# Attention with a condition, one core: the last step's scores move ahead of step 30's sums, and GpSimd adds half of them

## The chip, the core and the metric

The kernel runs on one core of a Trainium2 chip. Five engines work side by side, each through its own instructions in order, and wait for one another by semaphores: TensorE (PE in the profile, its weight loads PEld), VectorE (DVE), ScalarE (ACT), GpSimd (POOL) and SyncE (SP, which only issues DMAs). TensorE writes its results to PSUM, eight banks of 512 float32 columns; all else lies in SBUF. The metric is the device time of one execution in microseconds.

## The reference

For 8 sequences of 512 tokens and 512 features, 16 heads of 32 features each; everything is float32:

```python
Q, K, V = heads(x @ Wq.T + bq), heads(x @ Wk.T + bk), heads(x @ Wv.T + bv)
cQ = Q + heads(cond @ Wq.T + bq)
cK = K + heads(cond @ Wk.T + bk)
attn = softmax(cQ @ cK.T / sqrt(32))
out = x + merge(attn @ V)
```

A step of the kernel, `t` from 0 to 31, is one sequence and one group of four heads. For each it needs the scores, their row maxima, the exponentials, the sums of the exponentials (the softmax's denominators), the product of the exponentials with V, the division, and the addition of x.

## The kernel before

Only the last two steps bear on the change: `t = 30` and `t = 31`. Their scores are computed with the keys in the partitions. One call of `exponentials(t, kc, at)` makes the scores of one key block `kc` (128 keys, four heads j = 0 to 3, 512 queries): on TensorE four short matmuls that put minus the row maximum into four banks (L753, from the tile `maxT`), four that add keys times queries (L756), and on ScalarE four exponentials (L766), bank by bank in the order of `at`, into two buffers of `store`, one for heads 0 and 1 and one for heads 2 and 3. `crossed` (L1287) does the same for key blocks 0 to 2 of step 30 and makes maxima of step 31 in between; there the buffer of heads 2 and 3 is filled first.

`times_v(t, kc, pt)` multiplies such a block with V into one bank, four heads side by side (L824). The denominators need the sum of the exponentials over all keys. `sum_of(t, acc, kc, on, prs)` adds the buffers of key blocks elementwise on the engine `on`: for `kc = 1` block 0 plus block 1 (L1277), for `kc = 2` and `3` the tile `acc` plus that block (L1279). `prs` says which half, `[0]` (heads 0 and 1) or `[1]` (heads 2 and 3); one half is 128 x 1024 float32. `times_ones(acc, pd, ...)` then sums over the partitions by a matmul with ones (L850).

Step 31 can only begin once its row maxima stand as three bf16 parts in `split`: VectorE makes them by `split_max` (L715 to L718, 128 x 16 each), TensorE turns them (L737), VectorE copies them to `maxT` (L743). Behind that, each engine works in the order in which the code is written: TensorE takes turns between `exponentials` and `times_v`, VectorE runs the additions, ScalarE the exponentials.

At the very end, step 31's denominators and product are multiplied out on VectorE, turned on TensorE, divided, and sent out by two DMAs (L1442 to L1468). Step 30's result takes another way: the partial products are added in `parts` (L1403), VectorE turns the denominators (L1416) and the result (L1421), multiplies by the reciprocal (L1423), GpSimd adds x (L1424), and four DMAs send it (L1429).

The PSUM bank numbers in `at` matter as far as a bank that is to be written must have been read before.

Of the kernel before, what the change touches and what calls it, by code (L numbers as in the profile page):

```python
# [9 lines left out]
F32 = mybir.dt.float32  # L10
# [7 lines left out]
def kernel(  # L18
# [38 lines left out]
    nc = tc.nc  # L57
    P = 128
# [19 lines left out]
    op = ctx.enter_context(tc.tile_pool(name="op", bufs=2))  # L78
# [37 lines left out]
    def banks(i, n=1):  # L116

        row = row_of[0] or [at_end[j] for j in TURNS[turn[0]]]
        j = row[i]
        if n == 1:  # L120
            return psum[:, j, :]
        k = row[i + 1]
        return psum[:, j : k + 1 : k - j, :]

    def bank_of(i):
        return psum[:, at_end[i], :]
# [32 lines left out]
    BL = 32  # L159
    NB = S // BL  # L160
# [56 lines left out]
    def chunk():  # L217

        ring_at[0] += 1
        return store[:, places[(ring_at[0] - 1) % len(places)]]  # L220
# [366 lines left out]
    def open_max(t):  # L587
        if t not in nmax:
            nmax[t] = op.tile([P, NS, HG, 1], F32, tag="nmax", name=f"nmax_{t}", bufs=3)
            sums[t] = op.tile([P, NS, HG, 1], F32, tag="sums", name=f"sums_{t}", bufs=3)  # L590
# [48 lines left out]
    def row_scores(t, qc, j, pt):  # L639
        r = slice(j * HD, (j + 1) * HD)  # L640
        nc.tensor.matmul(  # L641
            pt,
            qkT["q", t][r, qc * P : (qc + 1) * P],
            qkT["k", t][r, :],
            start=True,
            stop=True,
        )

    def row_max_of(t, qc, pr, pt):
        nc.vector.tensor_reduce(  # L650
            nmax[t][:, qc, pr * 2 : pr * 2 + 2, 0], pt, AX.X, ALU.max, negate=True
        )
# [56 lines left out]
    def split_max(t, on=nc.gpsimd):  # L709

        if t >= T:
            return
        m, sp = nmax[t], split[t % 2]
        rest = op.tile([P, NS, HG, 1], F32, tag="rest", name=f"rest_{t}")
        on.tensor_copy(sp[:, :, :, 0:1], m)  # L715
        on.tensor_tensor(rest, m, sp[:, :, :, 0:1], ALU.subtract)
        on.tensor_copy(sp[:, :, :, 1:2], rest)
        on.tensor_tensor(sp[:, :, :, 2:3], rest, sp[:, :, :, 1:2], ALU.subtract)  # L718
# [29 lines left out]
    def exponentials(t, kc, at=None):  # L748

        bank = [bank_of(i) for i in at] if at else [banks(i) for i in range(HG)]  # L750
        for j in range(HG):
            r = slice(j * HD, j * HD + 3)
            nc.tensor.matmul(bank[j], onesb[r, :], maxT[t][r, :], start=True, stop=False)  # L753
        for j in range(HG):
            r = slice(j * HD, (j + 1) * HD)
            nc.tensor.matmul(  # L756
                bank[j],
                qkT["k", t][r, kc * P : (kc + 1) * P],
                qkT["q", t][r, :],
                start=False,  # L760
                stop=True,
            )
        for pr in range(NP):
            e = es[t, kc, pr] = chunk()
            for i in range(2):
                nc.scalar.activation(e[:, i, :], bank[pr * 2 + i], AF.Exp)  # L766
# [54 lines left out]
    def times_v(t, kc, pt, chunks=range(NS)):  # L821
        b, g = divmod(t, G)
        for j in range(HG):
            nc.tensor.matmul(  # L824
                pt[j * HD : (j + 1) * HD, :],
                vs[b % 2][:, kc, (g * HG + j) * HD : (g * HG + j + 1) * HD],
                es[t, kc, j // 2][:, j % 2, :],
                start=(kc == chunks[0]),
                stop=(kc == chunks[-1]),
            )  # L830
# [17 lines left out]
    def times_ones(of, pt, start, stop):  # L848
        for j in range(HG):
            nc.tensor.matmul(  # L850
                pt[j * HD : (j + 1) * HD, :],
                ones[:, :HD],
                of[j // 2][:, j % 2, :],
                start=start,
                stop=stop,
            )
# [100 lines left out]
    bank = bank_of  # L957
# [88 lines left out]
    parts = {}  # L1046

    def late_part(i):
        return late[0][:, i, :]
# [224 lines left out]
    def sum_of(t, to, kc, on, prs=range(NP)):  # L1274
        for pr in prs:
            if kc == 1:
                on.tensor_tensor(to[pr], es[t, 0, pr], es[t, 1, pr], ALU.add)  # L1277
            else:
                on.tensor_tensor(to[pr], to[pr], es[t, kc, pr], ALU.add)  # L1279

    def room_for_sums(t):
        a = stage.tile([P, NC, D], F32, tag="w", name=f"acc_{t}")
        return [a[:, pr * 2 : pr * 2 + 2, :] for pr in range(NP)]

    def row(i):
        turn[0] = 8 + i

    def crossed(t, kc, qc, u=None):


        u = u or t + 1
        open_max(u)
        bank = [banks(i) for i in range(HG)]

        def maxima(js):
            for j in js:
                row_scores(u, qc, j, banks(HG + j))

        def scores(js):
            for j in js:  # L1300
                r = slice(j * HD, j * HD + 3)
                nc.tensor.matmul(bank[j], onesb[r, :], maxT[t][r, :], start=True, stop=False)
            for j in js:
                r = slice(j * HD, (j + 1) * HD)
                nc.tensor.matmul(
                    bank[j],
                    qkT["k", t][r, kc * P : (kc + 1) * P],
                    qkT["q", t][r, :],
                    start=False,
                    stop=True,  # L1310
                )

        maxima((0, 1))
        scores((2, 3))
        scores((0, 1))
        maxima((2, 3))
        for pr in (1, 0):
            e = es[t, kc, pr] = chunk()
            for i in range(2):
                nc.scalar.activation(e[:, i, :], bank[pr * 2 + i], AF.Exp)  # L1320
        for j in range(2):
            nc.vector.tensor_reduce(
                nmax[u][:, qc, j : j + 1, 0], banks(HG + j), AX.X, ALU.max, negate=True
            )
        row_max_of(u, qc, 1, banks(HG + 2, 2))

    t = T - 3
# [46 lines left out]
    t = T - 2  # L1374
# [10 lines left out]
    acc = room_for_sums(t)  # L1385
    sum_of(t, acc, 1, nc.gpsimd, [1])
    part_of(t, banks(2), [0])
    row(2)
    crossed(t, 2, 3)
    split_max(t + 1, nc.vector)  # L1390
    pa, rest = banks(2), [1, 2, 3]
    times_v(t, 1, pa, rest)
# [2 lines left out]
    transpose_max(t + 1, bank(5), nc.vector.tensor_copy)  # L1395
    times_v(t, 2, pa, rest)
    sum_of(t, acc, 1, nc.vector, [0])
    sum_of(t, acc, 2, nc.vector)

    t = T - 1  # L1400
    exponentials(t, 0, (2, 3, 0, 1))
    times_v(t - 1, 3, pa, rest)
    nc.vector.tensor_tensor(parts[t - 1], pa, parts[t - 1], ALU.add)  # L1403
    sum_of(t - 1, acc, 3, nc.vector)
    exponentials(t, 1, (7, 4, 5, 2))
    pv = bank(3)
    times_v(t, 0, pv)
    acc2 = room_for_sums(t)
    sum_of(t, acc2, 1, nc.vector)
    exponentials(t, 2, (0, 1, 7, 6))  # L1410
    times_v(t, 1, pv)
    pd = bank(5)
    times_ones(acc, pd, True, True)
    sum_of(t, acc2, 2, nc.vector)
    den = late_part(3).rearrange("p (f e) -> p f e", e=BL)
    nc.vector.transpose(den.rearrange("p f e -> p (f e)"), pd)  # L1416

    rec = op.tile([P, NB, 1], F32, tag="recs", name=f"recs_{t - 1}")
    nc.vector.reciprocal(rec, den[:, :, 0:1])
    y30 = op.tile([P, NB, BL], F32, tag="res", name=f"res_{t - 1}")  # L1420
    nc.vector.transpose(y30.rearrange("p f e -> p (f e)"), parts[t - 1])  # L1421
    x30 = xr.pop(t - 1)
    nc.vector.tensor_tensor(y30, y30, rec.broadcast_to([P, NB, BL]), ALU.mult)  # L1423
    nc.gpsimd.tensor_tensor(y30, y30, x30, ALU.add)  # L1424
# [1 line left out]
    def store_30(queue, hs):  # L1426
        b, g = divmod(t - 1, G)
        for h in hs:
            queue.dma_start(spread(out[b], g * P + h * BL), y30[h * BL : (h + 1) * BL])  # L1429

    store_30(nc.sync, (0, 1))
    exponentials(t, 3, (4, 2, 0, 1))
    times_v(t, 2, pv)
    pd = bank(7)
    times_ones(acc2, pd, True, False)
# [66 lines left out]
```

## Time and profile before

| | us |
|---|---|
| median of 3 runs | 649.41 (649.35 to 650.63) |
| the profiled execution | 649.67 |
| its span in the trace | 647.80 |
| PE busy in the span | 641.7 (99%) |
| DVE busy | 600.3 (93%) |
| ACT busy | 533.5 (82%) |
| POOL busy | 409.9 (63%) |

The change touches only the last 25 us or so of the span, so that stage's own rows matter more than these shares. Of matmuls the profile models the end; they are pipelined, and two groups that follow each other overlap by a tenth or two of a microsecond in its rows.

### The profile page before, as it was taken

How to read it: one execution, taken by the hardware profiler on the slowest of the kernel's cores; microseconds unless marked ns; L12 is line 12 of the kernel's file. 1: busy time of each engine (PE TensorE's matmuls, PEld its weight loads, DVE VectorE, ACT ScalarE, POOL GpSimd, SP SyncE). 2: the span in 40 equal slices, each digit the busy share in tenths (PEclk: the TensorE clock that was granted, in tenths of full speed). 3: DMA queues.
4: the chain of work that ended last, by engine and by line, in shares of the span. 5: the costliest groups of instructions: out<-in, count | busy, mean ns of one | idle time of the engine just before them, and what ended most of it. 6: DMA issues, size and time to landing. Idle time of an engine off the chain costs nothing. (4 is left out here: it accounts for less than half of the span.)

```text
span 647.8 us, 24814 instructions
## 1 busy us (share of the span) xinstructions
PE 641.7 (99%) x9856; PEld 357.3 (55%) x9856; DVE 600.3 (93%) x845; ACT 533.5 (82%) x1364; POOL 409.9 (63%) x651
## 2 busy tenths in 40 slices
PE   9999999999999999999999999999999999999997
PEld 8445555556555555555555555555655555555541
DVE  3799999999999999999999999999999999999887
ACT  2479888889888889888888988898988888898564
POOL 3633655686765775668576776568767577675650
PEclk9999999999999999999999999999999999999999
DMA  7615588888978788877878978878898767796831
GB/s 191 107 26 85 128 164 171 172 171 191 180 158 172 161 180 175 183 165 164 185 171 174 198 150 185 165 173 169 180 195 158 156 144 163 159 189 149 192 63 34
DMA packets 248457, 102.02 MB, mean 157 GB/s; under 512 B 229962, under 2 KB 230474, under 8 KB 248340
## 3 DMA queue, kind: packets, MB, share of 16 engines
q1 hardware_dynamic: 234196, 65.54, 53.6%
q0 software_dynamic: 12384, 33.83, 20.3%
q8 instruction: 78, 1.28, 0.8%
q10 hardware_dynamic: 1760, 1.05, 0.5%
q14 instruction: 39, 0.32, 0.2%
HBM read 19.75 MB, written 8.39 MB: 43 GB/s over the span
## 5 line engine op out<-in xcount | busy, mean ns | idle before, releaser
L593 DVE TENSOR_REDUCE nmax<-psum 128x1 f32<-128x512 f32 x279 | 177.6, 675 | 9.2 <-PE psum L641 4.9
L701 ACT ACTIVATE psum<-psum,nmax 128x512 f32<-128x512 f32 x248 | 165.1, 678 | 3.6 <-DVE nmax L593 3.0
L641 PE MATMUL psum<-kT,qT 32*128 32x512 f32 x1024 | 162.0, 613 | 0.0
L701 ACT ACTIVATE store<-psum,nmax 128x512 f32<-128x512 f32 x204 | 139.5, 700 | 25.0 <-DVE nmax L593 24.8
L682 POOL DMA_DIRECT2D store<-store x258 | 128.6, 503 | 47.2 <-DMA store<-store 28.8
L799 ACT ACTIVATE store<-psum 128x512 f32<-128x512 f32 x232 | 119.8, 603 | 33.4 <-PE psum L785 33.4
L660 DVE STREAM_TRANSPOSE store<-store 128x1024 f32<-128x1024 f32 x116 | 138.9, 1217 | 0.0
L650 DVE TENSOR_REDUCE nmax<-psum 128x2 f32<-128x1024 f32 x98 | 118.9, 1213 | 0.0
L840 PE MATMUL psum<-store,v 128*32 128x256 f32 x1856 | 106.8, 381 | 0.2 <-ACT store L1320 0.2
L840 PEld LDWEIGHTS psum<-store,v 128*32 128x32 f32 x1856 | 57.3, 110 | 57.2 <-ACT wT_q L632 21.2
L913 POOL TENSOR_TENSOR res<-res,recs 128x512 f32<-128x512 f32 x30 | 31.3, 1045 | 90.8 <-DVE res L912 90.8
L785 PE MATMUL psum<-qT,kT 32*128 32x256 f32 x928 | 83.8, 374 | 0.0
L641 PEld LDWEIGHTS psum<-kT,qT 32*128 32x128 f32 x1024 | 61.6, 184 | 35.4 <-issue 17.8
L785 PEld LDWEIGHTS psum<-qT,kT 32*128 32x128 f32 x928 | 60.9, 184 | 5.6 <-issue 0.3
L701 ACT ACTIVATION_READ_ACCUMULATOR psum<-psum,nmax 128x1 f32 x248 | 55.1, 222 | 0.0
L203 POOL TENSOR_TENSOR xr<-xr,bvs 128x512 f32<-128x512 f32 x30 | 38.4, 1282 | 15.6 <-DMA x<-in_x_dram 12.8
L462 PE MATMUL psum<-wc_v,xc 128*32 128x256 f32 x768 | 47.7, 379 | 0.0
L462 PE MATMUL psum<-xc,wc_q 128*32 128x256 f32 x720 | 44.7, 379 | 0.0
L462 PE MATMUL psum<-xc,wc_k 128*32 128x256 f32 x720 | 44.5, 379 | 0.0
L701 ACT ACTIVATION_READ_ACCUMULATOR store<-psum,nmax 128x1 f32 x204 | 44.4, 217 | 0.0
L914 POOL TENSOR_TENSOR res<-res,xr 128x512 f32<-128x512 f32 x30 | 38.3, 1277 | 2.3
L462 PE MATMUL psum<-xT,wT_k 128*32 128x256 f32 x480 | 34.5, 382 | 0.0
(191 smaller groups left out, 972.5 us busy)
## 6 DMA issues: line engine op xcount, KB each, us to landing
store<-store SPq DMA_DIRECT2D x264, 128.0 KB, 2.6
store<-store POOLq DMA_DIRECT2D x258, 128.0 KB, 3.8
out_dram<-res SPq DMA_DIRECT2D x122, 64.0 KB, 3.6
xr<-in_x_dram SPq DMA_DIRECT2D x120, 64.0 KB, 4.4
x<-in_x_dram SPq DMA_DIRECT2D x112, 64.0 KB, 3.3
w_q<-in_L_cond_Wq_dram SPq DMA_DIRECT2D x4, 256.0 KB, 3.9
w_v<-in_L_cond_Wv_dram SPq DMA_DIRECT2D x16, 64.0 KB, 2.5
w_k<-in_L_cond_Wk_dram SPq DMA_DIRECT2D x16, 48.0 KB, 2.6
```

Source lines behind the costliest of these rows:

```text
L203: nc.gpsimd.tensor_tensor(xr[t], xr[t], bias, ALU.add)
L462: nc.tensor.matmul(pt[r], still[:, r], moving, start=(kc == kcs[0]), stop=(kc == kcs[-1]))
L593: nc.vector.tensor_reduce(nmax[t][:, qc, j : j + 1, 0], pt, AX.X, ALU.max, negate=True)
L641: nc.tensor.matmul(pt, qkT["q", t][r, qc * P : (qc + 1) * P], qkT["k", t][r, :], start=True, stop=True,)
L650: nc.vector.tensor_reduce(nmax[t][:, qc, pr * 2 : pr * 2 + 2, 0], pt, AX.X, ALU.max, negate=True)
L660: nc.vector.transpose(e, e)
L682: (nc.gpsimd if here else nc.sync).dma_start(to, of)
L701: nc.scalar.activation(to, of, AF.Exp, bias=nmax[t][:, qc, j, :], accum_out=sums[t][:, qc, j, :],)
L785: nc.tensor.matmul(banks(j)[:, i * HS : (i + 1) * HS], qkT["k", t][r, kc * P : (kc + 1) * P], qkT["q", t][r, KQ * P :], start=False, stop= ...
L799: nc.scalar.activation(e[:, j], banks(j), AF.Exp)
L840: nc.tensor.matmul(pt[j * HD : (j + 1) * HD, half * HS : (half + 1) * HS], vs[b % 2][:, kc, (g * HG + j) * HD : (g * HG + j + 1) * HD], e, ...
L914: nc.gpsimd.tensor_tensor(y, y, xr.pop(t), ALU.add)
```

## The change

Four things change in the last two steps.

1. Of step 30's additions `kc = 2` and `kc = 3`, the half `[1]` moves from VectorE to GpSimd, which already made that half of `kc = 1`. VectorE keeps the half `[0]` and makes it right behind its other additions of step 30.
2. The transposition of step 30's result (`y30`) moves on VectorE from behind the denominators' to right behind the addition of `parts`.
3. On TensorE (and so for ScalarE) the scores of the last key block, `exponentials(t, 3)` of step 31, move ahead of step 30's sums with ones and of the product `times_v(t, 2)`; step 30's sums with ones stand behind them.
4. The banks change with it: the last scores go to (4, 5, 2, 0) instead of (4, 2, 0, 1), step 30's sums to bank 1 instead of 5.

```diff
     part_of(t, banks(2), [0])
     row(2)
     crossed(t, 2, 3)
+    sum_of(t, acc, 2, nc.gpsimd, [1])
     split_max(t + 1, nc.vector)
     pa, rest = banks(2), [1, 2, 3]
     times_v(t, 1, pa, rest)
...
     transpose_max(t + 1, bank(5), nc.vector.tensor_copy)
     times_v(t, 2, pa, rest)
     sum_of(t, acc, 1, nc.vector, [0])
-    sum_of(t, acc, 2, nc.vector)
+    sum_of(t, acc, 2, nc.vector, [0])
+    sum_of(t, acc, 3, nc.vector, [0])
+    sum_of(t, acc, 3, nc.gpsimd, [1])
 
     t = T - 1
     exponentials(t, 0, (2, 3, 0, 1))
     times_v(t - 1, 3, pa, rest)
     nc.vector.tensor_tensor(parts[t - 1], pa, parts[t - 1], ALU.add)
-    sum_of(t - 1, acc, 3, nc.vector)
+    y30 = op.tile([P, NB, BL], F32, tag="res", name=f"res_{t - 1}")
+    nc.vector.transpose(y30.rearrange("p f e -> p (f e)"), parts[t - 1])
     exponentials(t, 1, (7, 4, 5, 2))
     pv = bank(3)
     times_v(t, 0, pv)
...
     exponentials(t, 2, (0, 1, 7, 6))
     times_v(t, 1, pv)
-    pd = bank(5)
+    sum_of(t, acc2, 2, nc.vector)
+    exponentials(t, 3, (4, 5, 2, 0))
+    pd = bank(1)
     times_ones(acc, pd, True, True)
-    sum_of(t, acc2, 2, nc.vector)
     den = late_part(3).rearrange("p (f e) -> p f e", e=BL)
     nc.vector.transpose(den.rearrange("p f e -> p (f e)"), pd)
 
     rec = op.tile([P, NB, 1], F32, tag="recs", name=f"recs_{t - 1}")
     nc.vector.reciprocal(rec, den[:, :, 0:1])
-    y30 = op.tile([P, NB, BL], F32, tag="res", name=f"res_{t - 1}")
-    nc.vector.transpose(y30.rearrange("p f e -> p (f e)"), parts[t - 1])
     x30 = xr.pop(t - 1)
...
     store_30(nc.sync, (0, 1))
-    exponentials(t, 3, (4, 2, 0, 1))
     times_v(t, 2, pv)
```

What stands in VectorE's row before, from the parts of step 31's maxima to the product of step 30's result with its reciprocal (`acc_8444` is step 30's sum, `acc_8540` step 31's, `x2` both halves):

```order
L715 CAST split<-nmax_8338 128x16
L716 TENSOR_TENSOR rest_8471<-nmax_8338,split 128x16
L717 CAST split<-rest_8471 128x16
L718 TENSOR_TENSOR split<-rest_8471,split 128x16
L743 COPY maxT_8496<-psum 128x512
L1277 TENSOR_TENSOR acc_8444<-store 128x1024
L1279 TENSOR_TENSOR acc_8444<-acc_8444,store 128x1024 x2
L1403 TENSOR_TENSOR parts<-psum,parts 128x512
L1279 TENSOR_TENSOR acc_8444<-acc_8444,store 128x1024 x2
L1277 TENSOR_TENSOR acc_8540<-store 128x1024 x2
L1279 TENSOR_TENSOR acc_8540<-acc_8540,store 128x1024 x2
L1416 STREAM_TRANSPOSE store<-psum 128x512
```

And the same place in the changed kernel, from the copy to `maxT` on (`acc_8542` is now step 31's sum, `res_8524` step 30's result):

```order
L743 COPY maxT_8497<-psum 128x512
L1277 TENSOR_TENSOR acc_8444<-store 128x1024
L1279 TENSOR_TENSOR acc_8444<-acc_8444,store 128x1024 x2
L1406 TENSOR_TENSOR parts<-psum,parts 128x512
L1408 STREAM_TRANSPOSE res_8524<-parts 128x512
L1277 TENSOR_TENSOR acc_8542<-store 128x1024 x2
L1279 TENSOR_TENSOR acc_8542<-acc_8542,store 128x1024 x2
L1421 STREAM_TRANSPOSE store<-psum 128x512
```

Five additions of step 30 have become three, all of the half `[0]`, and the transposition of the result stands ahead of step 31's additions.

GpSimd's row at its end, in the changed kernel, from the result of step 29 (`res_8417`) on; before, the row of L1279 was not there:

```order
L913 TENSOR_TENSOR res_8417<-res_8417,recs_8415 128x512
L914 TENSOR_TENSOR res_8417<-res_8417,xr_8143 128x512
L1277 TENSOR_TENSOR acc_8444<-store 128x1024
L1279 TENSOR_TENSOR acc_8444<-acc_8444,store 128x1024 x2
L1427 TENSOR_TENSOR res_8524<-res_8524,store 128x512
```

The two additions stand where GpSimd had nothing between L1277 and step 30's last addition.

## The prediction

> **What bounds the kernel now.** I read the page's shares first, then the chain of work that ended last, then the timeline of each engine in the last 25 us, where the change lies.
>
> ```profile
> PE 641.7 (99%) x9856; PEld 357.3 (55%) x9856; DVE 600.3 (93%) x845; ACT 533.5 (82%) x1364; POOL 409.9 (63%) x651
> ```
>
> TensorE is busy for nearly the whole span. So a wait that puts TensorE back before its last work is paid in full, unless a later wait swallows it. The chain, in order of time (start, length, what), says where TensorE isn't the bound:
>
> ```profile
> 638.23 1.24 DVE acc L1279
> 639.47 0.04 issue
> 639.51 1.48 PE psum L850 x10
> ```
>
> Its last passage from VectorE to TensorE is VectorE's last addition of step 31 (L1279, `kc = 2`, half `[1]`), which releases the sums with ones (L850). From there to the end the chain is a fixed sequence. TensorE's timeline shows that wait (start, length, what):
>
> ```profile
> 634.47 1.07 PE L824 MATMUL psum<-store,v 128*32 128x512 f32 x8
> 635.36 1.04 PE L850 MATMUL psum<-acc,ones 128*32 128x512 f32 x8
> ...
> 637.52 1.07 PE L824 MATMUL psum<-store,v 128*32 128x512 f32 x8
> 638.40 1.73 PE L850 MATMUL psum<-acc,ones 128*32 128x512 f32 x6
> 639.52 0.62 PE L850 MATMUL psum<-store,ones 128*32 128x512 f32 x2
> ...
> 640.82 0.60 PE L850 MATMUL psum<-store,ones 128*32 128x512 f32 x2
> ```
>
> A group of eight starts 0.88 after the one before (637.52 to 638.40) and takes 1.04. The sums of step 31 are two groups, so without a wait they would end at 638.40 + 0.88 + 1.04 = 640.32. They end at 640.82 + 0.60 = 641.42: VectorE costs **1.1 us** here. That is all that a faster VectorE can give, as TensorE's timeline has no gap from L737's turning (627.59, below) to 638.40.
>
> VectorE in the same stretch has no idle time that matters until the sums are there:
>
> ```profile
> 628.09 0.42 DVE L743 COPY maxT<-psum 128x512 bf16<-128x512 bf16 x1 [0.56 <-ACT store L766]
> 628.43 1.22 DVE L1277 TENSOR_TENSOR acc<-store 128x1024 f32<-128x1024 f32 x1
> 629.68 2.36 DVE L1279 TENSOR_TENSOR acc<-acc,store 128x1024 f32<-128x1024 f32 x2
> 631.96 0.69 DVE L1403 TENSOR_TENSOR parts<-psum,parts 128x512 f32<-128x512 f32 x1
> 632.56 2.35 DVE L1279 TENSOR_TENSOR acc<-acc,store 128x1024 f32<-128x1024 f32 x2
> 634.83 2.36 DVE L1277 TENSOR_TENSOR acc<-store 128x1024 f32<-128x1024 f32 x2
> 637.10 2.36 DVE L1279 TENSOR_TENSOR acc<-acc,store 128x1024 f32<-128x1024 f32 x2
> 639.37 0.72 DVE L1416 STREAM_TRANSPOSE store<-psum 128x512 f32<-128x512 f32 x1
> 640.12 0.25 DVE L1419 RECIPROCAL recs<-store 128x16 f32<-128x16 f32 x1
> 640.29 0.71 DVE L1421 STREAM_TRANSPOSE res<-parts 128x512 f32<-128x512 f32 x1
> 641.04 0.69 DVE L1423 TENSOR_TENSOR res<-res,recs 128x512 f32<-128x512 f32 x1
> 642.11 0.69 DVE L1443 TENSOR_TENSOR store<-psum,xT 128x512 f32<-128x512 f32 x1 [0.38 <-ACT store L1442]
> ```
>
> An addition of one half takes 1.22; independent ones start 1.135 apart (634.83 to 637.10 is two), one that needs the result just before it 1.25 (628.43 to 629.68).
>
> **The change part by part.** First what it removes, as if nothing else happened. Two additions leave VectorE (2.27), the transposition of the result comes in ahead of step 31's additions (0.6). But step 31's additions also wait for ScalarE:
>
> ```profile
> 624.35 2.07 ACT L1320 ACTIVATE store<-psum 128x512 f32<-128x512 f32 x4 [0.64 <-PE psum L1305]
> 627.47 2.07 ACT L766 ACTIVATE store<-psum 128x512 f32<-128x512 f32 x4 [1.05 <-PE psum L756]
> 630.19 6.44 ACT L766 ACTIVATE store<-psum 128x512 f32<-128x512 f32 x12 [0.66 <-PE psum L756]
> 637.67 2.06 ACT L766 ACTIVATE store<-psum 128x512 f32<-128x512 f32 x4 [1.04 <-PE psum L756]
> 641.49 0.58 ACT L1442 COPY store<-psum 128x512 f32<-128x512 f32 x1 [1.76 <-PE psum L850]
> ```
>
> Twelve exponentials in 6.44 end some 0.53 apart; the sixth, which the first addition of step 31 needs, at 633.45, the twelfth at 636.63. VectorE's new row is then: three dependent additions from 628.43, 629.68 and 630.93, `parts` 632.07, transposition 632.79, and step 31's four additions from 633.5, so that the last ends at 633.5 + 3 x 1.135 + 1.22 = 638.1, instead of 639.46. On TensorE the last scores and step 30's sums change places, the same matmuls in the same time, so step 31's sums are still due at 638.40. They would not wait: **the gain is the 1.1 us** above. The earlier scores let ScalarE begin its last four exponentials at 636.6 instead of 637.67, so they end by 638.8, ahead of 639.28, when the sums over them begin. That hides the move; left where they were they would end at 639.73 and cost some 0.4. The banks cost nothing: 4, 5 and 2 are read by 634.5 and bank 0 by 635.2, the new place is behind 635.36, and bank 1 is read an exponential after bank 0. The two stores on SP and the two behind ScalarE's copy keep their queues; step 30's result, off the chain, follows VectorE.
>
> Then what it adds: two additions on GpSimd. Their price and their place:
>
> ```profile
> 623.75 2.35 POOL L1277 TENSOR_TENSOR acc<-store 128x1024 f32<-128x1024 f32 x1
> 641.81 1.28 POOL L1424 TENSOR_TENSOR res<-res,store 128x512 f32<-128x512 f32 x1 [15.70 <-DVE res L1423]
> ```
>
> GpSimd is idle from 626.10 to 641.81. The addition of block 2 has its input by 625.4 (the half `[1]` is filled first in ScalarE's row of 624.35), so it **runs from 626.1 to 628.5**; block 3 has its input when ScalarE's row of 627.47 ends, so it **runs from 629.6 to 632.0**. Both are long ready for step 30's sums, now due a block of scores later, at 635.36 + (637.52 - 635.36 - 0.88) = 636.64. By readiness alone nothing is lost. But look at what VectorE does beside them:
>
> ```profile
> 625.36 1.21 DVE L650 TENSOR_REDUCE nmax<-psum 128x2 f32<-128x1024 f32 x1
> ...
> 626.84 0.19 DVE L716 TENSOR_TENSOR rest<-nmax,split 128x16 f32<-128x16 f32 x1
> ...
> 627.30 0.23 DVE L718 TENSOR_TENSOR split<-rest,split 128x16 bf16<-128x16 f32 x1
> ```
>
> ```profile
> 627.59 0.40 PE L737 MATMUL psum<-identb,split 128*128 128x128 bf16 x4 [0.21 <-DVE split L718]
> ```
>
> L716 and L718 have two inputs from SBUF, and so have the additions. In this stretch of the trace of before GpSimd's arithmetic never lies beside such an instruction of VectorE: beside L1277 VectorE reduces PSUM (L650), and from 626.1 to 641.81 GpSimd is still. So the price of the meeting isn't shown, and I bound it. At the low end they don't notice each other. The nearest row for that is GpSimd issuing DMAs beside the same L716, which takes its usual 0.18:
>
> ```profile
> 612.44 1.52 POOL L682 DMA_DIRECT2D store<-store  x3
> 613.36 0.18 DVE L716 TENSOR_TENSOR rest<-nmax,split 128x16 f32<-128x16 f32 x1
> ```
>
> At the high end VectorE's instruction waits until GpSimd's, which was first, is over: up to 2.35 each time, the row of L1277. **I take the high end.** It is nearer in kind: the low end's row issues descriptors and adds nothing, L1277 is the very operation. And VectorE adds two streams of 1024 in 1.22, the time in which it transposes one (1.217 on average, below), so it draws both at once, where GpSimd takes 2.35 for the same two, as though it had one way in. That the second stream of VectorE comes by GpSimd's way is possible by these rows, and not shown by them.
>
> ```profile
> L660 DVE STREAM_TRANSPOSE store<-store 128x1024 f32<-128x1024 f32 x116 | 138.9, 1217 | 0.0
> ```
>
> The Trainium skill, page "SBUF — State Buffer", section "Who interferes with whom", speaks against this change: a VectorE instruction with two SBUF inputs fetches the second through an interface that it shares with GpSimd's reads; whichever issues first keeps it for its whole instruction, and the other stands still. By that rule the sum comes out at the high end, without it at 1.1 us less than before. No run here has shown it yet; L660, with one input, has GpSimd's arithmetic beside it through most of the span and stays at a mean of 1217 ns, which the rule allows.
>
> **The sum, at the high end.**
> 1. L716 would start at 626.84 and waits until 628.49: 1.65 later. L717 and L718 follow, `split` is ready at 629.18. Behind L716 stands VectorE's whole row; on TensorE the turning L737 starts at 629.24 instead of 627.59, and all of TensorE's row behind it moves by 1.65.
> 2. L743 (from PSUM) ends at 630.17. Block 3 on GpSimd started at 629.6 (its scores stand ahead of L737, so it isn't late), so VectorE's first addition waits until 632.0 instead of starting at 630.1.
> 3. From 632.0: three dependent additions (632.0, 633.25, 634.5), `parts` 635.64, transposition 636.36, then four additions at 636.98, 638.11, 639.25 and 640.38. The last ends at 641.60; before it was 637.10 + 2.36 = 639.46. ScalarE, 1.65 later, is ready at 638.3 and doesn't set this.
> 4. TensorE reaches step 31's sums at 638.40 + 1.65 = 640.05 and waits, as before, for that addition. From there the sequence to the end is the same: **+2.14 us**. Step 30's result needs 0.72 + 0.25 + 0.69 more on VectorE, to some 643.2, ahead of L1443 at 644.25, so it stays hidden.
>
> The profiled execution took 649.67: 649.67 + 2.14 = 651.81. It lies 0.26 above the median of the runs shown, so against the median I give **651.6**.
>
> **The rivals.**
> - *The engines don't notice each other.* Then the 1.1 us come out whole: 649.67 - 1.1 - 0.26 = 648.3, which is 0.17% less. For it: L716 beside the DMA descriptors. Against: that is no read of tensors. It decides for the other side, not slower, if L718 still ends at 627.5.
> - *Only the long additions collide.* The small L716 slips in, TensorE is on time, VectorE's first addition starts at 628.5. GpSimd's block 3 asks at 629.6 and comes next, until 632.07; then 632.1, 633.35, `parts` 634.5, 635.2, 635.8 and three more, end 640.44: +0.98, 650.4. If the two share evenly and each is only slowed, VectorE loses some 1.2 of the 1.36 that it had won: 649.4.
> - *The change doesn't do what it says.* GpSimd's half might be late for the sums: it would have to end after 636.64, over 4 us late, and nothing in the rows makes it so, unless VectorE holds GpSimd back through all its additions; that would still leave a part of the first rival.
>
> **How the numbers follow.** Full waiting 0.55, the half cases 0.15, no meeting 0.30. The first lies over 0.2% (1.3 us, about what a measurement of this kernel can tell from no change) above 649.41, from 651.1 to 652.5 if each release costs a little or one wait is shorter. The half cases are within 0.2%. Of the third, a little under half would fall below 648.1: 0.13. So faster 0.13, within 0.2% 0.32, slower 0.55. Both signs hold much of the chance, so the range spans 648.0 to 652.5; the likeliest case alone 651.1 to 652.5.
>
> **What would show it.** Right: L716 stretched, or begun at about 628.5; L737 near 629.2; VectorE's first addition of step 30 beginning, or lasting, to 632 or more; its last of step 31 ending near 641.6. Wrong: L718 done at 627.5 with GpSimd busy beside it; additions of VectorE at 1.22 beside GpSimd's; or GpSimd's additions stretched well over 2.35 instead, with VectorE on time. Step 31's sums on TensorE without a gap would mean the 1.1 us were won.

## The result, and the profile after

| | before | changed |
|---|---|---|
| median of 5 runs, us | 649.50 (649.35 to 650.63) | 652.70 (652.15 to 653.57) |
| ratio | 1 | 1.0044, 95% interval 1.0033 to 1.0055 |
| the profiled execution, us | 649.67 | 652.15 |
| its span in the trace, us | 647.8 | 650.4 |

The kernel became slower by 0.3 to 0.6%. The forecast of 651.6 against 649.41 was a ratio of 1.0034, inside that interval. The median itself lies 0.2 above the range's upper end of 652.5. Timed again (below), the same kernel took 652.07, with a ratio of 1.0030.

GpSimd's timeline of the changed kernel (start, length, what, and in brackets the idle time before it):

```profile
624.12 2.36 POOL L1277 TENSOR_TENSOR acc<-store 128x1024 f32<-128x1024 f32 x1
626.55 2.34 POOL L1279 TENSOR_TENSOR acc<-acc,store 128x1024 f32<-128x1024 f32 x1
630.05 2.36 POOL L1279 TENSOR_TENSOR acc<-acc,store 128x1024 f32<-128x1024 f32 x1 [1.15 <-ACT store L766]
```

L1277 stands ahead of everything that changed and starts at 624.12 instead of 623.75. So this execution was already **0.37** late for reasons outside the change, and I take 0.37 off each time below that is compared with before. The two new additions lie where the prediction put them and take their usual 2.35.

VectorE's timeline of the changed kernel in the same columns:

```profile
626.98 1.98 DVE L715 CAST split<-nmax 128x16 bf16<-128x16 f32 x1
629.00 0.18 DVE L716 TENSOR_TENSOR rest<-nmax,split 128x16 f32<-128x16 f32 x1
629.21 0.20 DVE L717 CAST split<-rest 128x16 bf16<-128x16 f32 x1
629.45 0.23 DVE L718 TENSOR_TENSOR split<-rest,split 128x16 bf16<-128x16 f32 x1
630.24 0.42 DVE L743 COPY maxT<-psum 128x512 bf16<-128x512 bf16 x1 [0.56 <-PE psum L737]
630.58 2.91 DVE L1277 TENSOR_TENSOR acc<-store 128x1024 f32<-128x1024 f32 x1
633.53 2.56 DVE L1279 TENSOR_TENSOR acc<-acc,store 128x1024 f32<-128x1024 f32 x2
636.00 0.68 DVE L1406 TENSOR_TENSOR parts<-psum,parts 128x512 f32<-128x512 f32 x1
636.78 0.71 DVE L1408 STREAM_TRANSPOSE res<-parts 128x512 f32<-128x512 f32 x1
637.41 2.32 DVE L1277 TENSOR_TENSOR acc<-store 128x1024 f32<-128x1024 f32 x2
639.65 2.35 DVE L1279 TENSOR_TENSOR acc<-acc,store 128x1024 f32<-128x1024 f32 x2
```

Before, the first of the split's casts (conversions to bf16) stood there as:

```profile
626.61 0.20 DVE L715 CAST split<-nmax 128x16 bf16<-128x16 f32 x1
```

Now this cast of 16 columns takes 1.98 and ends at 628.96, when GpSimd's addition has just ended (626.55 + 2.34 = 628.89). An addition that took 1.22 takes 2.91 and ends at 633.49. GpSimd's second addition ended at 632.41 and VectorE's 1.08 later, a little less than its own length of 1.22, so nearly all of it was made behind GpSimd's. The waiting shows as a long instruction, not as idle time. The last addition of step 31 ends at 639.65 + 2.35 = 642.00. Without the 0.37 that is 641.63, against 639.46 before: **+2.17**, where the prediction had +2.14.

TensorE's timeline of the changed kernel, from the turning of the maxima on:

```profile
629.74 0.40 PE L737 MATMUL psum<-identb,split 128*128 128x128 bf16 x4 [1.98 <-DVE split L718]
630.07 1.07 PE L824 MATMUL psum<-store,v 128*32 128x512 f32 x8
631.06 0.55 PE L753 MATMUL psum<-maxT,onesb 3*128 3x512 bf16 x4
631.39 1.93 PE L756 MATMUL psum<-qT,kT 32*128 32x512 f32 x8
633.25 1.71 PE L824 MATMUL psum<-store,v 128*32 128x512 f32 x8
...
641.33 1.04 PE L824 MATMUL psum<-store,v 128*32 128x512 f32 x8
642.19 1.04 PE L850 MATMUL psum<-acc,ones 128*32 128x512 f32 x8
643.05 1.04 PE L850 MATMUL psum<-store,ones 128*32 128x512 f32 x8
```

There is one gap, of 1.98 instead of 0.21, ahead of L737. Behind it a group of scores (L756) takes 1.93; before, the same group was:

```profile
629.14 1.03 PE L756 MATMUL psum<-qT,kT 32*128 32x512 f32 x8
```

The sums of step 31 (L850) begin at 642.19, and the group ahead of them began 0.86 before, so they wait for nothing. They end at 643.05 + 1.04 = 644.09, without the 0.37 at 643.72, against 641.42 before: **+2.30**. The spans differ by 2.6, a little less than 0.37 + 2.30 = 2.67: the last store is issued 2.74 later (647.16 after 644.42), and the span ends 3.2 behind it instead of 3.4.

The chain of work that ended last (start, length, what) takes another way than before:

```profile
626.98 1.99 DVE split L715
...
631.61 1.71 PE psum L756 x8
...
642.37 1.84 PE psum L850 x16
```

From the turning of the maxima at 629.74 to the end of the sums it stays on TensorE without a break. Up to there it holds VectorE's cast, and none of VectorE's additions of exponentials.

The windows of the changed kernel say why the scores are long (stretch and its length; busy time and count of each engine; then the clock that TensorE was granted, as a share of the full clock, the DMA share and GB/s):

```profile
629.70:631.00 1.30, 1.26 (x12) 0.38 (x12) 0.76 (x2) 0.21 (x1) 0.95 (x1) 1.00 0.00 0
631.00:632.00 1.00, 1.00 (x12) 0.62 (x12) 1.00 (x1) 0.00 (x0) 1.00 (x1) 0.59 0.00 0
632.00:633.30 1.30, 1.30 (x12) 0.05 (x8) 1.30 (x1) 0.00 (x0) 0.41 (x1) 0.50 0.00 0
633.30:634.90 1.60, 1.60 (x15) 0.17 (x13) 1.46 (x3) 1.56 (x4) 0.00 (x0) 0.59 0.00 0
634.90:638.20 3.30, 3.30 (x36) 0.96 (x32) 3.21 (x4) 2.53 (x6) 0.00 (x0) 1.00 0.01 2
```

For some 3.4 us the granted clock is halved, and the matmuls take about twice their time. This the prediction didn't have. So the result left three questions: do GpSimd's halves cause the loss, do the cast and the addition really wait for GpSimd, and what does the halved clock cost?

### The profile page after: what moved, and what is told of

It reads as the page before. It is cut to its first block, busy times and chain, and to the rows that moved or that the text cites. A ratio compares the mean times of both kernels' runs of the same rounds, so it can differ in the third digit from the quotient of the medians.

```text
span 650.4 us, 24815 instructions
## 1 busy us (share of the span) xinstructions
PE 643.1 (99%) x9856; PEld 358.3 (55%) x9856; DVE 601.6 (93%) x843; ACT 533.5 (82%) x1364; POOL 414.5 (64%) x653
## 3 DMA queue, kind: packets, MB, share of 16 engines
q8 instruction: 78, 1.28, 0.8%
## 4 chain that ended last, share of the span: by engine, by line
PE 98%; DVE 1%; issue 0%; ACT 0%; DVEq 0%
PE psum L462 44%; PE psum L641 18%; PE psum L840 16%; PE psum L785 8%; PE psum L772 3%; PE psum L405 2%; PE psum L824 2%; PE psum L756 1%; PE psum L956 0%; PE psum L850 0%; PE psum L753 0%; PE psum L313 0%; PE psum L359 0%; DVE split L715 0%; PE psum L934 0%; PE psum L1305 0%
```

## The experiments

My theory: VectorE's cast and its first addition wait for GpSimd's additions. The rivals: the moved scores and the moved transposition cost the time; the halved clock costs it; any work of GpSimd, reading or not, slows VectorE.

**The moves without the halves.** All additions of step 30 stay on VectorE, in the changed kernel:

```diff
-    sum_of(t, acc, 2, nc.gpsimd, [1])
...
-    sum_of(t, acc, 2, nc.vector, [0])
-    sum_of(t, acc, 3, nc.vector, [0])
-    sum_of(t, acc, 3, nc.gpsimd, [1])
+    sum_of(t, acc, 2, nc.vector)
+    sum_of(t, acc, 3, nc.vector)
```

> The changed kernel with all additions of step 30 but GpSimd's first one back on VectorE; the other moves stay. Theory (VectorE's instructions with SBUF inputs wait for GpSimd's additions): the first part of the split takes 0.20 again, TensorE's gap before L737 is 0.2, its clock stays 1.0; VectorE has its old row plus the transposition of the result (0.6) ahead of step 31's additions, so about 0.6 over the kernel before, 650.1. Rival (the moved scores or the moved transposition are what costs): it stays near 652.7.

It took 650.25, a ratio of 1.0009 (0.9999 to 1.0018): nearly all of the loss is gone. The cast takes 0.20 again, and the clock stays whole. TensorE's timeline of this kernel shows something else:

```profile
635.21 0.37 PE L753 MATMUL psum<-maxT,onesb 3*128 3x512 bf16 x1 [1.28 <-DVE parts L1404]
...
640.30 1.23 PE L850 MATMUL psum<-acc,ones 128*32 128x512 f32 x8
```

The scores of key block 2 go to banks 0, 1, 7 and 6 in turn, and bank 6 holds the products that VectorE adds into `parts`. Here that addition stands behind five additions of step 30, so TensorE waits 1.28 for its fourth bank. This is a second passage from VectorE to TensorE, which the prediction didn't look at.

**The halves without the moves.** The kernel before, with only the lines on GpSimd and VectorE's `[0]` halves from the diff:

```diff
+    sum_of(t, acc, 2, nc.gpsimd, [1])
...
-    sum_of(t, acc, 2, nc.vector)
+    sum_of(t, acc, 2, nc.vector, [0])
+    sum_of(t, acc, 3, nc.vector, [0])
+    sum_of(t, acc, 3, nc.gpsimd, [1])
...
-    sum_of(t - 1, acc, 3, nc.vector)
```

> The kernel before with nothing changed but the two halves that GpSimd adds. Theory: the same two stalls as in the changed kernel (first part of the split about 2.0, first addition of step 30 near 2.9) and the same slow stretch of TensorE; the last scores come later, so 652.2 to 653. Rival (the moves cost): no worse than the kernel before, 648.5 to 649.5.

It took 651.9, a ratio of 1.0038 (1.0027 to 1.0050). VectorE's timeline of it has both waits:

```profile
626.34 2.00 DVE L715 CAST split<-nmax 128x16 bf16<-128x16 f32 x1
...
629.96 2.89 DVE L1277 TENSOR_TENSOR acc<-store 128x1024 f32<-128x1024 f32 x1
```

The halves alone cost nearly what the whole change costs. In the profiled execution TensorE also waits 0.89 for `parts`, and its clock is whole behind a gap of 2.00. So the loss doesn't need a halved clock.

**Each half alone.** In the changed kernel, first only block 2's half on GpSimd, then only block 3's:

```diff
-    sum_of(t, acc, 3, nc.vector, [0])
-    sum_of(t, acc, 3, nc.gpsimd, [1])
+    sum_of(t, acc, 3, nc.vector)
```

> The changed kernel with the half of block 3 back on VectorE: GpSimd's addition of block 2 alone, so only the split meets it. Theory: cast 1.98 and TensorE's gap before L737 2.0 as in the changed kernel, VectorE's first addition 1.22 again; VectorE has one addition more than there but doesn't wait for the second, so its last addition ends some 1.2 to 1.4 later than in the kernel before; time 650.8 to 651.6, up to 652 where the clock is halved behind the gap. Rival (nearly all of the loss comes from the first meeting): 652 or more.

```diff
-    sum_of(t, acc, 2, nc.gpsimd, [1])
...
+    sum_of(t, acc, 2, nc.vector, [1])
     sum_of(t, acc, 2, nc.vector, [0])
```

> The changed kernel with the half of block 2 on VectorE, and only that of block 3 on GpSimd, behind it: the split meets nothing. Theory of taking turns: GpSimd asks while an addition of VectorE runs and waits for its end, then holds VectorE's next addition for some 2.3 (that one's row about 3.3 long); the split takes its old times; TensorE has no gap before L737 but one of 2.5 to 2.7 ahead of the scores of key block 2, which wait for the addition of parts; VectorE's last addition ends some 1.7 later than in the kernel before; 651 to 652.5. Rival (VectorE has the right of way when it asks without a break): the addition stays 1.22 and GpSimd's becomes long; 649.5 or less.

Block 2's half alone took 651.68, a ratio of 1.0030 (1.0018 to 1.0042). In its profile the cast takes 1.99, the additions their 1.22, and the clock is whole. But that execution, at 650.82, is the shortest of the six. Two of them, 650.82 and 651.11, have a mean granted clock of 1.000; the other four, 651.63 to 652.47, have 0.996 to 0.997, and 3.4 us at half the clock would lower the mean of such a span by 0.003. So here, where VectorE's last addition ends only 640.87 + 0.14 - 639.46 = 1.55 later than before (the execution was 0.14 early by GpSimd's L1277), a halved clock seems to cost about 1 us. It isn't shown to lie behind this gap, as only one execution was profiled.

Block 3's half alone took 652.51, a ratio of 1.0045 (1.0031 to 1.0059). There the cast takes 0.20 and the additions wait. GpSimd's, VectorE's and TensorE's rows from the timelines of this second kernel:

```profile
631.22 3.22 POOL L1279 TENSOR_TENSOR acc<-acc,store 128x1024 f32<-128x1024 f32 x1 [4.80 <-ACT store L766]
```

```profile
632.31 3.21 DVE L1279 TENSOR_TENSOR acc<-acc,store 128x1024 f32<-128x1024 f32 x1
```

```profile
636.17 0.37 PE L753 MATMUL psum<-maxT,onesb 3*128 3x512 bf16 x1 [2.20 <-DVE parts L1406]
636.18 1.90 PE L756 MATMUL psum<-qT,kT 32*128 32x512 f32 x8
638.00 1.94 PE L824 MATMUL psum<-store,v 128*32 128x512 f32 x8
```

GpSimd asks while VectorE's addition runs and takes 3.22 instead of 2.36: it too waits for the other. VectorE's next addition waits behind it and takes 3.21, `parts` comes late, TensorE waits 2.20 for bank 6, and the clock halves behind that gap. So each kernel with one meeting costs about as much as the one with both. That is not the price of one meeting alone, as VectorE makes one addition more in each of them (some 1.13).

**The split on GpSimd.** If only the cast's wait mattered, it would help to let GpSimd make the split itself, ahead of its addition:

```diff
+    split_max(t + 1, nc.gpsimd)
     sum_of(t, acc, 2, nc.gpsimd, [1])
-    split_max(t + 1, nc.vector)
```

> The changed kernel with step 31's split on GpSimd, ahead of its first new addition, so that the split meets no addition. Theory: TensorE's gap before L737 falls from 2.0 to about 0.5 and its clock stays 1.0 (L756 x8 in 1.03 instead of 1.93); VectorE's additions still meet GpSimd's, the first waits until about 630.3, a later one may wait another 2.3; its last addition ends 0.5 to 2.5 later than before, 650 to 652. If the slow stretch of TensorE has another cause than the gap, L756 x8 takes 1.9 again.

This missed: 653.96, a ratio of 1.0064 (1.0049 to 1.0079). TensorE is on time, L737 waits only 0.53. But GpSimd's two additions now stand back to back beside VectorE's three:

```profile
627.44 5.68 POOL L1279 TENSOR_TENSOR acc<-acc,store 128x1024 f32<-128x1024 f32 x2
```

```profile
628.42 2.48 DVE L1277 TENSOR_TENSOR acc<-store 128x1024 f32<-128x1024 f32 x1
630.93 4.61 DVE L1279 TENSOR_TENSOR acc<-acc,store 128x1024 f32<-128x1024 f32 x2
```

GpSimd's first ends at 629.81, VectorE's first at 630.90 (1.09 later), GpSimd's second at 633.12 (2.22 later), VectorE's second at 634.21 (1.09 later). The engines take turns, one whole addition each; nothing is shared out within one. TensorE then waits 2.52 for `parts`, and the clock halves again.

**The gap filled.** To price the halved clock, nine matmuls on ones, whose results nothing uses, stand ahead of the turning in the changed kernel:

```diff
+    for _ in range(9):
+        nc.tensor.matmul(bank(5), onesb, maxT[t], start=True, stop=True)
     transpose_max(t + 1, bank(5), nc.vector.tensor_copy)
```

> The changed kernel with nine more matmuls of ones on TensorE (results unused) in the gap before L737. Theory (the halved clock comes from the gap, but VectorE's lateness alone would cost nearly as much): the clock stays 1.0, TensorE reaches step 31's sums 1.6 sooner and waits there for VectorE's last addition; time 0.1 to 0.4 under the changed kernel, 652.3 to 652.6. Rival (TensorE's slow stretch sets the time): 1.6 under it, 651.1. Second rival (the slow stretch doesn't come from the gap): L756 x8 still takes 1.9.

It took 651.99, a ratio of 1.0035 (1.0022 to 1.0048), which can't be told from the changed kernel's. Its clock is whole behind L737, and its timelines on TensorE and VectorE show where the time went instead:

```profile
631.20 1.03 PE L756 MATMUL psum<-qT,kT 32*128 32x512 f32 x8
...
636.69 0.37 PE L753 MATMUL psum<-maxT,onesb 3*128 3x512 bf16 x1 [0.95 <-DVE parts L1408]
...
641.78 1.28 PE L850 MATMUL psum<-acc,ones 128*32 128x512 f32 x8
```

```profile
639.60 2.35 DVE L1279 TENSOR_TENSOR acc<-acc,store 128x1024 f32<-128x1024 f32 x2
```

With a whole clock TensorE waits 0.95 for `parts` and then, within its sums, for VectorE's last addition, which ends at 641.95. The sums end at 642.64 + 1.28 = 643.92, and this execution was 0.26 late ahead of the change (GpSimd's L1277 at 624.01), so at 643.66, against 643.72 with the halved clock. The chain that ended last, as far as the profile follows it back, begins with the L753 that waited for `parts`. The slow clock had only hidden these waits: VectorE was as late.

**The changed kernel again**, to see whether the halved clock comes back:

> The changed kernel once more, for a second profile. The stalls on VectorE should come again to within 0.05 (first part of the split 1.98, first addition 2.91). Open is TensorE's halved clock behind the gap before L737: it came in the changed kernel's profile (gap 1.98), not with GpSimd's halves alone (gap 2.00). If a gap of 2.0 always halves it, L756 x8 takes 1.9 again; if it does so only sometimes, L756 may take 1.03, and then TensorE waits some 0.9 for the addition of parts before the scores of key block 2. Time 652 to 653 in both cases, as VectorE's last addition sets the end nearly alike.

It took 652.07 (651.38 to 652.32), a ratio of 1.0030 (1.0016 to 1.0043). The cast takes 1.99, the gap is 1.99, and the clock halves again, this time directly behind the gap: the first group of L824 behind L737 takes 1.94.

The mean granted clock of every execution says more than the two profiles. Of the ten executions of the changed kernel, five have a mean of 0.993 to 0.997, the two profiled ones among them, and took 651.38 to 653.57. The other five have 0.999 to 1.000, as the kernel before has (0.998 to 1.000), and took 652.07 to 652.70. So the halved stretch seems to come in only half of the executions, and those without it are no faster.

**What of GpSimd's work disturbs.** In the kernel of the first experiment, GpSimd fills a buffer that nothing reads with six memsets, at the place of its first addition:

```diff
+    for _ in range(6):
+        nc.gpsimd.memset(parts["idle"], 0.0)
```

> All of step 30's additions but the first on VectorE, and GpSimd writes six memsets of 128 x 1024 into unused memory in the place of its two additions. First theory (VectorE's second input comes by the way by which GpSimd reads): a GpSimd that only writes stops no addition; each takes 1.22, the split's subtractions 0.19 and 0.23; the casts of the split (one input, SBUF to SBUF), which the changed kernel shows waiting too, may still wait. Rival (any GpSimd instruction stops VectorE's work on SBUF): the additions beside the memsets are stretched.

One execution gave 650.88, beside 649.8 for the kernel before. GpSimd's and VectorE's timelines:

```profile
626.01 2.97 POOL L1392 MEMSET parts<- 128x1024 f32 x3
```

```profile
626.56 0.47 DVE L715 CAST split<-nmax 128x16 bf16<-128x16 f32 x1
627.06 0.18 DVE L716 TENSOR_TENSOR rest<-nmax,split 128x16 f32<-128x16 f32 x1
627.28 0.75 DVE L717 CAST split<-rest 128x16 bf16<-128x16 f32 x1
...
629.19 1.21 DVE L1278 TENSOR_TENSOR acc<-store 128x1024 f32<-128x1024 f32 x1
```

The memsets only write. L716, with two inputs, and the long addition lie beside them at their usual lengths. Both casts wait until a memset ends (three in 2.97, so one at about 627.0, one at 628.0).

Then three multiplications by a constant, which read one half of a block and write the same unused buffer:

```diff
+    for _ in range(3):
+        nc.gpsimd.tensor_scalar(parts["idle"], es[t, 2, 1], 2.0, None, ALU.mult)
```

> The same with three GpSimd multiplications by a constant (one input of 128 x 1024 from SBUF) instead of the memsets. If reading is what collides, the cast and the additions of VectorE wait for each of them whole, as for the additions: the first cast about as long as the first multiplication, and VectorE and GpSimd take turns. If only instructions with two inputs collide: nothing is stretched.

One execution gave 654.5, with TensorE waiting 2.84 for `parts`, as VectorE's later additions meet the other multiplications. The same two timelines:

```profile
625.61 2.79 POOL L1392 TENSOR_SCALAR parts<-store 128x1024 f32<-128x1024 f32 x1
```

```profile
626.12 0.58 DVE L715 CAST split<-nmax 128x16 bf16<-128x16 f32 x1
626.74 0.18 DVE L716 TENSOR_TENSOR rest<-nmax,split 128x16 f32<-128x16 f32 x1
...
629.58 6.18 DVE L1280 TENSOR_TENSOR acc<-acc,store 128x1024 f32<-128x1024 f32 x4
```

The multiplication lasts until 628.40, but the cast is through at 626.70, 1.1 after its start, and L716 lies beside the rest of it unhindered. So VectorE doesn't always wait for GpSimd's whole instruction: with the one input, the cast, which alone takes 0.20, waited for about the first 0.9 of 2.79, with the two inputs of the addition for nearly all of 2.35. The additions wait here too: the four of L1280 take 6.18, beside 4.63 in the kernel without GpSimd's work.

**Is there a version that beats both?** Two attempts without GpSimd's halves. In the kernel before, the addition of `parts` moves behind step 31's additions and the last scores ahead of step 30's sums, with banks chosen so that nobody waits for `parts`. In the first the product with the reciprocal also moves to GpSimd (the last two lines); the second leaves it on VectorE:

```diff
-    nc.vector.tensor_tensor(parts[t - 1], pa, parts[t - 1], ALU.add)
...
-    exponentials(t, 2, (0, 1, 7, 6))
+    exponentials(t, 2, (0, 1, 7, 4))
...
+    sum_of(t, acc2, 2, nc.vector)
+    exponentials(t, 3, (5, 2, 0, 1))
+    pd = bank(7)
     times_ones(acc, pd, True, True)
-    sum_of(t, acc2, 2, nc.vector)
+    nc.vector.tensor_tensor(parts[t - 1], pa, parts[t - 1], ALU.add)
...
-    nc.vector.tensor_tensor(y30, y30, rec.broadcast_to([P, NB, BL]), ALU.mult)
+    nc.gpsimd.tensor_tensor(y30, y30, rec.broadcast_to([P, NB, BL]), ALU.mult)
```

> A version without GpSimd's halves: the kernel before, with the addition of parts taken out of VectorE's row ahead of step 31's additions (it goes behind them, so its bank stays taken and the last two blocks of scores use other banks), the scores of the last block ahead of step 30's sums, and the product of step 30's result with its reciprocal on GpSimd. If VectorE's last addition is what the kernel before waits for, it ends 0.6 sooner, TensorE still waits some 0.5, and the time is 0.6 less: 648.9, ratio 0.999. If the new banks are read too late, TensorE loses 0.2 and the gain is 0.4. Rival (the end is set by something else): 649.5 or more.

> As the version with parts late, but the product of step 30's result with its reciprocal on VectorE again, so that step 30's last stores don't stand ahead of the last DMA on ScalarE's queue. If those stores ate the 0.6 us there, some 0.3 to 0.4 comes out here: 649.2 to 649.4, ratio 0.9994. Rival (the last DMAs' landing sets the end whatever comes before): ratio 1.000.

They took 650.05, a ratio of 1.0002 (0.9993 to 1.0011), and 649.6, a ratio of 0.9997 (0.9988 to 1.0006); one of the second's eleven executions took 1669.67 and isn't counted. Neither showed the gain that was expected. In the first, VectorE's last stretch starts earlier than before (L1443 at 641.78, less the 0.27 by which this execution was late 641.51, before 642.11). But the last store is issued on ScalarE's queue at 644.82 - 0.27 = 644.55 instead of 644.42, behind two stores of step 30 that had become late. With the product back on VectorE it is issued at 644.32, less 0.18 at 644.14. Neither differs from the kernel before by more than the intervals hold.

## Why the prediction was right, and where it wasn't

- **The meeting, and its price.** Right. Both meetings happened at the predicted places. The first addition was to end at 632.0 + 1.25 = 633.25 and ended at 633.49 - 0.37 = 633.12; step 31's last was put at 641.60 and ended at 641.63. That the halves cause it is shown by taking them out (1.0009) and by putting them in alone (1.0038).
- **Step 1, the instruction.** "L716 would start at 626.84 and waits until 628.49": L716 took 0.18. It was the cast ahead of it, L715, with one input, that waited, and ended at 628.96 - 0.37 = 628.59. I had looked only for instructions with two inputs. The Trainium skill, page "SBUF — State Buffer", section "Who interferes with whom", also lists casts among the operations that can, under conditions on their operands, take the pair of ports for reading and writing that VectorE shares with GpSimd. The runs agree: the casts waited for memsets, the two-input instructions did not. The end of the row is hardly changed by this, since both stand at the same place.
- **Step 1, what is behind it.** "All of TensorE's row behind it moves by 1.65" fell short. L737 moved by 1.78 (629.74 - 0.37 - 627.59), but what follows moved further. The step left out two things. The first is the wait for `parts`: TensorE wants bank 6 for the last of four short matmuls (L753), some 0.3 into a group that began at 633.29 before, so by the prediction's own shift at about 633.29 + 0.3 + 1.65 = 635.2. The prediction started `parts` at 635.64, which with its 0.69 is done at 636.3. So its own numbers held a wait of 1.1, and it didn't look; 0.95 was measured with the gap filled. The second is the halved clock, which put the same time elsewhere.
- **Step 4, who ends last.** "TensorE reaches step 31's sums at 638.40 + 1.65 = 640.05 and waits": it reached them at 642.19 - 0.37 = 641.82 and didn't wait. That the end came out right to 0.2 (+2.30 for +2.14) is because VectorE's last addition, at 641.63, was nearly as late. With the gap filled TensorE waited for VectorE after all, for `parts` and within its sums, and these ended at the same time. So the sum was right by VectorE's row, and the account of TensorE's was not. That TensorE's own delay, of which the sum has only the 1.65, came within 0.2 of VectorE's is luck.
- **The rivals.** That the engines don't notice each other fell: every kernel with such a meeting showed it. That only the long additions collide fell with the cast (1.98). That they share evenly fell with the turns of whole additions. That GpSimd's half comes too late fell too: it ended at 632.41, and step 30's sums began at 640.45. What the removal alone would have won (the 1.1 us of the first rival) wasn't tried: no kernel here takes those additions off VectorE without giving them to GpSimd.
- **The range.** 652.5 was 0.2 too low for the first median and held the second, 652.07. The intervals of the two ratios overlap; what lies between the two medians isn't explained.

## What to carry to other kernels

Before work goes to GpSimd because it is idle there, read VectorE's row over the whole time of GpSimd's instruction: an addition of GpSimd stopped VectorE's casts and two-input additions until it was over, so in the two profiles of the changed kernel each meeting cost 1.5 to 1.8, where the half itself had cost VectorE 1.22. Such a wait is found by comparing lengths with those of the same line elsewhere, as it shows in no list of waits. And follow each delayed engine to all that it releases, the freeing of PSUM banks too: here one addition late in a row held a bank that TensorE wanted.

## What the runs showed of the hardware

- **TensorE's clock halves behind gaps of 2 us, not always.** In the profiles, gaps of 1.98 and 1.99 (the changed kernel twice), 2.20 and 2.52 were followed by a granted clock of 0.50 for 3.4 us, and one of 2.84 by 6.8 us of it; gaps of 2.00 (the halves alone) and 1.99 (block 2's half alone) were not, nor were those up to 1.28. The Trainium skill, page "TensorE: Matmul & The Clock Gate", in its Part 1, puts the fall behind an idle window of about 3.4 us; here it came behind shorter gaps. The mean clocks of the changed kernel's executions and of those with block 2's half alone suggest that the same kernel halves it in some executions and not in others. What decides it stays open.
- **Casts wait for GpSimd's writes, two-input additions only where it reads**: 0.47 and 0.75 for casts of 0.20 beside memsets, 0.18 and 1.21 for the others, in one profile.
- **How long GpSimd holds VectorE depends on its instruction**: nearly all of 2.35 for an addition, about 0.9 of 2.79 for a multiplication by a constant, in one profile. That VectorE waits until GpSimd's instruction is over, as the prediction's high end has it, fits the addition and not this multiplication.
